# Where a block's statistics stand, and which engine fills its buffers with ones

## The chip, the cores and the metric

The kernel runs on one core of a Trainium2 chip. A core has five engines with a queue of their own each, and each works its queue off in order: TensorE (PE, with the weight loads shown apart as PEld), VectorE (DVE), ScalarE (ACT), GpSimd (POOL) and SyncE (SP, which here only issues transfers). They wait for each other by semaphores. The metric is the device time of one execution in microseconds. Three runs of the kernel before took 902.11 to 902.88 us, median 902.47.

## The reference

The input x has 2 batches of 2048 rows of 256 features, all in float32. Each row is normalised, and an attention and a spectral layer, both of the normalised row, are added to it:

```python
xn = _layernorm(x, axis=-1)
x = x + _L0_attn_ref(xn, wq, wk, wv, wo) + _L0_ffn_ref(xn, w_freq_real, w_freq_imag, bias)
```

The attention has 16 query heads of 16 features and 4 key and value heads, with a rotary embedding on queries and keys and a causal mask:

```python
scores = jnp.einsum('bshd,bthd->bhst', q, k) * scale
scores = jnp.where(causal[None, None, :, :], scores, -jnp.inf)
attn = jax.nn.softmax(scores, axis=-1)
out = jnp.einsum('bhst,bthd->bshd', attn, v).reshape(Bx, Sx, Dx) @ wo
```

The spectral layer is the real part of an inverse FFT of (FFT of xn) times a complex matrix, plus a bias. For a given matrix that is one real 256 x 256 matrix.

## The kernel before, in words

**Blocks and units.** The rows are cut into 8 blocks of 512. The blocks of the two batches alternate: block 0 and block 1 are the first 512 rows of either batch, block 2 and 3 the second, and so on. A unit is one block with one group of 4 query heads, one for each key head, so there are 32 units. Units 0 to 3 belong to block 0, 4 to 7 to block 1, 8 to 11 to block 2. Because of the causal mask later blocks see more key blocks, and their units are longer.

**The way of one block to its scores.** `load_x` brings in the rows (tile `xt`, four row tiles of 128). `row_stats` takes mean and variance of one row tile on VectorE with two instructions (`bn_stats`, `bn_aggr`; lines 283 and 284, tiles `bn` and `mv`). `row_power` makes 1/sqrt(variance + eps) on GpSimd (lines 289, 290, tile `rs`), `row_shift` the shift on VectorE (line 295, tile `sh`). `norm` applies both, four instructions (line 445). `transpose_x` turns the rows over on TensorE (banks `ps_x`, copied by ScalarE to `xnT`), `features` multiplies with the weights (banks `ps_q`, copied to `raw`), for the keys and values first (c = 2), then for two halves of the queries (c = 0 and 1). `other_half` swaps the halves of each head for the rotation: for blocks 0 and 1 by a product (banks `ps_sw`), from block 2 on by transfers. `rotate` and `split` are seven instructions for each c: three for the rotation with the table `cs`, four that split the result into three bf16 parts (tile `part`: high, middle, low). For block 0 they run on VectorE, for the other blocks on GpSimd; the same holds for `norm`. `stack` and `stack_runs` copy the parts by transfers from SyncE's queue (line 439) into `kst` (keys) and `qst` (queries of a unit), seven times 16 partitions, so that one bf16 product over 112 partitions adds up the products of parts.

**Ones.** `ones(n)` fills two buffers of block n before they are partly overwritten: `va[n]` with 1.0 (line 419; values overwrite half of the columns, and a column of ones gives the softmax sums), and the partitions 96 to 127 of `kst[n]` with -1.0, one instruction for each of the four key heads (line 422; the rows 112 to 114 subtract the row maxima).

**The two passes.** First come the row maxima of a unit (`maxima`): TensorE makes score tiles (banks `sm` for whole key blocks, `sd` for the diagonal one, in a ring of two), and VectorE reduces them (line 681), the last of a unit followed by `parts` (lines 792 to 808, tile `np_of`), which turns the maxima into bf16 parts. `spread` brings them to the stacked queries. Then `scores` makes transposed scores with the maximum already taken off (banks `st` or `sp`), ScalarE takes the exponential (line 952, tile `es`), `values` multiplies with `va` (bank `av`), and sums and products go through memory (`put`, `gather`, `widen`) to `output`.

**The spectral matrix.** `spectral_matrix` makes the real matrix on TensorE from tables that `load_late` brings in by GpSimd's queue: four pieces `left` (banks `ps_ff`), then two `right` (banks `ps_mff`).

**What sets the order.** The program is written out at build time by a planner. It keeps a clock for each engine in `clock`, and the time at which each thing will be there in `there`. `use(engine, us, needs, gives)` advances a clock. Work that is not scores, values or maxima stands in `streams`, lists of pieces with the engine, what they need, and two places in the order (from when they may and by when they should be issued). The loop at the end picks what can start soonest, by these estimates, and prefers late maxima. A piece whose needs are not yet in `there` is not picked. So a change of one estimate or one need can change the order in which all engines get their work. At run time only this order and the semaphores count.

**The start.** Before the loop, 48 idle transposes go to TensorE, then the planner's clocks are set (line 1226), and block 0 gets its ones, statistics, `row_power`, the loads of `load_late`, the rotary table (`rotary_table`, line 339) and its shift. `chain(n, ...)` puts the pieces of block n into streams; for blocks 0 and 1 and for block 2's load they may be issued at once. The statistics of block 2 may be issued early too, as its place in the order is before the start:

Of the kernel before, what the change touches and what calls it, by code (L numbers as in the profile page):

```python
# [23 lines left out]
def tile_attn_plus_spectral_ffn(  # L24
# [29 lines left out]
    nc = tc.nc  # L54
# [35 lines left out]
    clock = {e: 0.0 for e in ("pe", "dve", "act", "pool", "sp")}  # L90
# [36 lines left out]
    def use(eng, us, needs=(), gives=()):  # L127
        clock[eng] = max(clock[eng], ready(needs)) + us
        if eng == "pe":
            at = issued[0] // LOADED  # L130
            for k in range(max(loaded), at + 1):
                clock["pe"] = max(clock["pe"], loaded[k])
                loaded[k + 1] = clock["pe"] + LOAD
            clock["pe"] = max(clock["pe"], loaded[at])
        for k in gives:
            there[k] = clock[eng] + LATE[eng]
# [46 lines left out]
    xt = {}  # L183

    def load_x(n):
        at = slot("xt")
        take_slot("xt")
        xt[n] = work.tile([P, NI, D], F32, tag="xt", bufs=2, name=f"xt{n}")
        step = NI if n else 1
        for i in range(0, NI, step):  # L190
            send("sp", 128 * step, [at], [("xt", "in", n, k) for k in range(i, i + step)])
            nc.sync.dma_start(out=xt[n][:, i : i + step, :], in_=block_rows(n)[:, i : i + step, :])
# [86 lines left out]
    def row_stats(n, i):  # L279
        if i == 0:  # L280
            mv[n] = work.tile([P, NI, 2], F32, tag="mv", bufs=2, name=f"mv{n}")
        st = work.tile([P, 6], F32, tag="bn", bufs=3, name=f"bn{n}_{i}")
        nc.vector.bn_stats(st, xt[n][:, i, :])
        nc.vector.bn_aggr(mv[n][:, i, :], st)
        use("dve", 0.6, [("xt", "in", n, i)], [("mv", n)])

    def row_power(n):
        rstd[n] = work.tile([P, NI], F32, tag="rs", bufs=2, name=f"rs{n}")
        nc.gpsimd.tensor_scalar(rstd[n], mv[n][:, :, 1], EPS, None, ALU.add)
        nc.gpsimd.tensor_tensor(rstd[n], rstd[n], neg_half, ALU.pow)  # L290
        use("pool", 1.6, [("mv", n)], [("rs", n)])

    def row_shift(n):
        shift[n] = work.tile([P, NI], F32, tag="sh", bufs=2, name=f"sh{n}")
        nc.vector.scalar_tensor_tensor(
            shift[n], mv[n][:, :, 0], -1.0, rstd[n], ALU.mult, ALU.mult
        )
        use("dve", 0.2, [("rs", n)], [("sh", n)])
# [115 lines left out]
    xnT, va, kst, qst = {}, {}, {}, {}  # L414

    def ones(n):
        e, eng, us = (nc.vector, "dve", 2.7) if n == 0 else (nc.gpsimd, "pool", 2.9)
        va[n] = const.tile([P, NI, NKV, QD], F32, tag=f"va{n}", name=f"va{n}")
        e.memset(va[n], 1.0)
        kst[n] = const.tile([P, NKV, SB], BF16, tag=f"kst{n}", name=f"kst{n}")  # L420
        for h in range(NKV):
            e.memset(kst[n][96:P, h, :], -1.0)
        use(eng, us, (), [("ones", n)])
# [791 lines left out]
    def stream(pieces, since=-1, by=-1):  # L1215
        streams.append([(since, by, *p) for p in pieces])
        return streams[-1]
# [5 lines left out]
    for _ in range(48):  # L1223
        transpose(idle[:, 0:P], ident, ident)
    use("pe", 9.0, (), [("st", k)])
    clock["dve"], clock["act"], clock["pool"] = 1.8, 3.7, 1.8
    ones(0)
    for i in range(NI):
        row_stats(0, i)
# [7 lines left out]
    def chain(n, starts, late=0):  # L1237

        norms, pe, rot = project(n)
        eng = norms[0][0]  # L1240
        stats = [("dve", [("xt", "in", n, i)], [], lambda i=i: row_stats(n, i)) for i in range(NI)]
        stats.append(("pool", [("mv", n)], [], lambda: row_power(n)))
        stats.append(("dve", [("rs", n)], [], lambda: row_shift(n)))
        s = starts
        if n > 1:
            stream([("sp", [], ["xt"], lambda: load_x(n))], s["load"], s["load"])
        if n:
            norm_1 = [("xn", 1, NI - 1)]
            stream([("pool", norm_1, [], lambda: ones(n))], s["ones"], s["stats"])
            stream(stats, s["stats"], s["stats"] + late + 1)  # L1250
        out_pe = streams.append([]) or streams[-1]
        for k, p in enumerate(pe):
            at = s["pe"] + (k // 2 if n > 1 else 0)
            out_pe.append((at, at + late + 1, *p))
        out_rot = streams.append([]) or streams[-1]
        for p in norms:
            out_rot.append((s["stats"], s["stats"] + late + 2, *p))
        for c, more in ((K, 0), (Q0, 2), (Q1, 5)):
            at = s["rot"] + (more if n > 1 else 0)
            for k, p in enumerate(rot[c]):  # L1260
                out_rot.append((at, at + late + 2 + k // 2, *p))
# [10 lines left out]
    early = dict.fromkeys(("load", "ones", "stats", "pe", "rot"), -1)  # L1272
    table(0, -1)
    chain(0, early, -9)
    chain(1, early, 1)
    load_x_2 = stream([("sp", [], ["xt"], lambda: load_x(2))])

# [5 lines left out]
    for n in range(2, NB):  # L1283
        at = next(k for k, d in enumerate(due) if d >= a_from[NG * n])
        starts = dict(load=at - 30, stats=at - 24, pe=at - 20, rot=at - 17)
        starts["ones"] = 0 if n < 4 else 8 * n - 26
        if n == 2:
            starts["load"] = -1
        if n % B == 0:
            table(n // B, max(at - 22, 2))  # L1290
        chain(n, starts)
# [65 lines left out]
    while True:  # L1357
# [4 lines left out]
        if now < NS:  # L1362
            u, t = steps[now]
            h = b_next % NKV
            n, g = units[u]
# [20 lines left out]
        for s in streams:  # L1386
            if s and (s[0][0] <= now or now >= NS):
                since, by, eng, needs, rings, what = s[0]
# [11 lines left out]
        if others and min(others, key=lambda c: c[0])[0] <= limit:  # L1400
            soonest = min(others, key=lambda c: c[0])
            eng = soonest[1][0][2]
# [12 lines left out]
        act, dve = clock["act"] - pe, clock["dve"] - pe  # L1415
# [21 lines left out]
        if kind == "B":  # L1437
# [3 lines left out]
            if b_next % NKV == 0 and first[u + 1] == now + 1:  # L1441
                n, g = units[u]
# [71 lines left out]
```

## Time and profile before

| | |
|---|---|
| median of three runs | 902.47 us |
| the profiled execution | 901.48 us, its span 899.8 us |
| PE busy | 881.7 us, 98% |
| DVE busy | 731.0 us, 81% |
| ACT busy | 638.1 us, 71% |
| POOL busy | 363.3 us, 40% |
| chain that ended last | PE 88%, DVE 8%, ACT 2% |

All times in the profile are microseconds from the start of the span. A line of the timeline gives start, duration, engine, source line, operation and tiles; several alike are merged with a count, and the bracket tells how long the engine had been idle and what ended that. In the table by stage each engine's busy time in a stretch is followed by its number of instructions; the last three columns are the granted clock of TensorE, the busy share of the DMA engines and GB/s. The chain that ended last is followed backwards from the last instruction, at each step to what released it. Matmuls overlap in the pipeline and their ends are modelled, so a full PE need not be a PE at its peak. The granted clock is 1.00 in all stretches.

### The profile page before, as it was taken

What the parts mean: (1) busy time and instruction counts of PE and PEld (TensorE: products, weight loads), DVE (VectorE), ACT (ScalarE), POOL (GpSimd) and SP (SyncE); (2) the same over time, 40 slices, a digit from 0 to 9 for tenths busy, and PEclk for the clock granted to TensorE, in tenths of its full rate; (3) what the DMA queues carried; (4) which work ended last, traced back from release to release, by engine and by line L of the source; (5) the groups of instructions that cost most, each with busy time, mean ns of one, the idle gap of its engine ahead of it and who ended that gap; (6) DMA issues with size and microseconds to landing.
All of it is one profiled execution on the core that took longest, in us unless ns stands there. A gap on an engine that the chain in (4) does not pass through costs nothing.

```text
span 899.8 us, 37181 instructions
## 1 busy us (share of the span) xinstructions
PE 881.7 (98%) x16620; PEld 477.7 (53%) x16620; DVE 731.0 (81%) x1007; ACT 638.1 (71%) x1191; POOL 363.3 (40%) x486
## 2 busy tenths in 40 slices
PE   8899899999999999999999999999999999999998
PEld 5467664555555555555555555555455554545443
DVE  8886997968879996899987899979889989798501
ACT  3365756857767883978964987858597887579885
POOL 6968467725842325712255431212651111101111
PEclk9999999999999999999999999999999999999999
DMA  5446523531343012430012610010143001100000
GB/s 170 116 136 171 148 87 101 134 108 45 79 139 94 29 40 58 128 106 15 15 45 70 167 40 14 26 39 14 53 108 74 14 3 39 50 14 15 27 2 25
DMA packets 42063, 62.02 MB, mean 69 GB/s; under 512 B 8920, under 2 KB 32200, under 8 KB 41904
## 3 DMA queue, kind: packets, MB, share of 16 engines
q1 hardware_dynamic: 32480, 41.18, 16.9%
q0 software_dynamic: 8128, 17.69, 6.2%
q8 instruction: 130, 2.13, 1.0%
q10 hardware_dynamic: 1296, 0.79, 0.3%
q14 instruction: 29, 0.24, 0.1%
HBM read 32.75 MB, written 18.40 MB: 57 GB/s over the span
## 4 chain that ended last, share of the span: by engine, by line
PE 88%; DVE 8%; ACT 2%; issue 1%; POOL 0%; ACTq 0%; POOLq 0%; DVEq 0%
PE av L121 25%; PE st L121 23%; PE sm L121 18%; PE sd L121 7%; PE po L121 6%; PE ps_q L121 4%; DVE top_g L681 2%; PE sp L121 2%; DVE mx L681 2%; ACT es L952 2%; PE ps_ff L121 1%; PE ps_x L125 1%; DVE np_of L808 1%; PE ps_m L121 0%; PE ps_sw L121 0%
## 5 line engine op out<-in xcount | busy, mean ns | idle before, releaser
L952 ACT ACTIVATE es<-st 128x512 f32<-128x512 f32 x1006 | 532.1, 607 | 142.7 <-PE st L121 122.5
L681 DVE TENSOR_REDUCE mx<-sm 128x2 f32<-128x1024 f32 x384 | 450.2, 1218 | 40.9 <-PE sm L121 39.9
L121 PE MATMUL st<-qst,kst 115*32 115x512 bf16 (+9 forms) x4744 | 340.0, 345 | 0.5 <-issue 0.2
L121 PE MATMUL av<-es,va 128*32 128x512 f32 (+3 forms) x2560 | 288.2, 529 | 0.4 <-ACT avs L1033 0.2
L121 PE MATMUL sm<-kst,qst 112*32 112x512 bf16 x3072 | 236.1, 379 | 1.5 <-DVE mx L681 0.8
L121 PEld LDWEIGHTS <-kst 115*32 115x32 bf16 x5120 | 162.4, 95 | 141.4 <-issue 64.6
L121 PEld LDWEIGHTS <-qst 112*32 112x32 bf16 x5632 | 151.7, 96 | 127.3 <-issue 81.2
L681 DVE TENSOR_REDUCE top_g<-sd 128x25 f32<-128x800 f32 (+1 forms) x192 | 168.3, 906 | 39.3 <-PE sd L121 38.8
L970 POOL TENSOR_SCALAR_AFFINE_SELECT es<-es 128x512 f32<-128x512 f32 (+1 forms) x120 | 65.3, 546 | 240.1 <-ACT es L952 239.9
L121 PEld LDWEIGHTS av<-es,va 128*32 128x32 f32 x2560 | 82.4, 109 | 46.7 <-issue 18.3
L121 PE MATMUL sd<-kst,qst 112*32 112x384 bf16 (+11 forms) x2560 | 101.6, 256 | 1.6 <-DVE top_g L681 1.4
L1044 POOL DMA_DIRECT2D res<-avs x30 | 18.0, 599 | 109.9 <-ACT avs L1023 109.9
L121 PEld LDWEIGHTS <-ident_h 128*32 128x32 bf16 x1344 | 47.4, 96 | 28.1 <-issue 21.9
L1158 DVE TENSOR_TENSOR xr<-po,xr 128x256 f32<-128x256 f32 x36 | 15.2, 424 | 48.8 <-PE po L121 48.3
L121 PE MATMUL sd<-mask,ident_h 128*32 128x64 bf16 x1024 | 53.7, 193 | 0.8 <-DVE mx L681 0.5
L121 PE MATMUL ps_q<-xnT,wp 128*32 128x512 f32 x384 | 47.3, 594 | 0.2 <-ACT xnT L460 0.2
L475 ACT COPY raw<-ps_q 128x512 f32<-128x512 f32 x24 | 14.1, 586 | 44.4 <-PE ps_q L121 42.8
L952 ACT ACTIVATE es<-sp 128x1024 f32<-128x1024 f32 x41 | 39.7, 1028 | 6.1 <-PE sp L121 5.9
L566 POOL TENSOR_TENSOR ra<-raw,cs 128x512 f32<-128x512 f32 (+1 forms) x21 | 27.3, 1300 | 20.1 <-ACT raw L475 19.2
L121 PE MATMUL po<-wo_sb,attT 128*32 128x256 f32 x512 | 34.3, 380 | 0.0
L121 PE MATMUL po<-mff,xnT 128*32 128x256 f32 x512 | 33.7, 379 | 0.0
L1069 POOL DMA_DIRECT2D sums<-den x15 | 8.1, 540 | 53.7 <-DVE den L1063 53.7
(115 smaller groups left out, 625.1 us busy)
## 6 DMA issues: line engine op xcount, KB each, us to landing
qst<-run SPq DMA_DIRECT2D x62, 128.0 KB
res<-avs POOLq DMA_DIRECT2D x30, 256.0 KB, 2.9
run<-part SPq DMA_DIRECT2D x31, 192.0 KB
qst<-run SPq DMA_DIRECT2D x31, 192.0 KB
xr<-in_L_attn_x_dram SPq DMA_DIRECT2D x16, 256.0 KB
sw<-raw SPq DMA_DIRECT2D x60, 64.0 KB
attT<-res POOLq DMA_DIRECT2D x15, 256.0 KB, 4.2
inv<-sums POOLq DMA_DIRECT2D x15, 256.0 KB, 3.7
```

What stands on the lines that cost most here:

```text
L121: nc.tensor.matmul(to, lhsT, rhs, **more)
L125: nc.tensor.transpose(to, of, unit)
L475: nc.scalar.copy(raw[c], ps)
L566: e.tensor_tensor(ra[c][:r], raw[c][:r], cs[j][:r, 0, :], ALU.mult)
L681: nc.vector.tensor_reduce(out, of, AX.X, ALU.max)
L808: nc.vector.tensor_reduce(to, of, AX.X, op, negate=negate)
L952: nc.scalar.activation(to, of, AF.Exp, scale=SCALE)
L970: nc.gpsimd.affine_select(out=to, in_=to, pattern=pattern, compare_op=ALU.is_ge, fill=0.0, base=0, channel_multiplier=-1,)
L1044: nc.gpsimd.dma_start(out=res[n, c][f], in_=avs[u])
L1069: nc.gpsimd.dma_start(out=sums, in_=den[n, c])
L1158: nc.vector.tensor_tensor(xr[n, r][:, e, :], po, xr[n, r][:, e, :], ALU.add)
```

## The change

Three things are changed. `ones(0)` runs on GpSimd, as it does for the other blocks, with an estimate of 2.5 us. The planner's clocks of VectorE and GpSimd at the start are set to 3.0 and 3.5 instead of 1.8. And the first row tile's statistics of block 2 need the maxima of the first unit, `("np", 0, 0)`, which are there after `parts` of unit 0; the other three row tiles stand behind it in the same stream. No computation is added or left out.

```diff
     def ones(n):
-        e, eng, us = (nc.vector, "dve", 2.7) if n == 0 else (nc.gpsimd, "pool", 2.9)
+        e, eng, us = nc.gpsimd, "pool", 2.5 if n == 0 else 2.9
...
-    clock["dve"], clock["act"], clock["pool"] = 1.8, 3.7, 1.8
+    clock["dve"], clock["act"], clock["pool"] = 3.0, 3.7, 3.5
     ones(0)
...
         stats = [("dve", [("xt", "in", n, i)], [], lambda i=i: row_stats(n, i)) for i in range(NI)]
+        if n == 2:
+            stats[0] = ("dve", [("xt", "in", n, 0), ("np", 0, 0)], [], lambda: row_stats(n, 0))
         stats.append(("pool", [("mv", n)], [], lambda: row_power(n)))
```

In the built program the order then differs from before in these places. On VectorE the five fills are gone, and the eight statistics instructions of block 2 stand between the first maxima of unit 1. On GpSimd the five fills stand ahead of block 0's `row_power`; block 2's `row_power` stands behind the first half of block 1's queries, its `norm` inside the second half. On TensorE block 2's `transpose_x` stands among the maxima of unit 2 instead of ahead of the first maxima, and the four `ps_ff` pieces stand one ahead of `ps_sw` of block 1's keys, one among unit 0's maxima, one in unit 1's and one in unit 2's; before, two stood in units 0 and 1 and two behind unit 4's. Later differences are exchanges of neighbours, and from the fourth key tile of unit 16 on the order on TensorE is the same.

## The prediction

> **What bounds the kernel now.** I read the page's shares first, then busy time by stage, then the start instruction by instruction, then the chain of waits.
>
> ```profile
> PE 881.7 (98%) x16620; PEld 477.7 (53%) x16620; DVE 731.0 (81%) x1007; ACT 638.1 (71%) x1191; POOL 363.3 (40%) x486
> ```
>
> Busy time by stage (columns: stretch, length, then PE, PEld, DVE, ACT, POOL):
>
> ```profile
> 0.00:31.00 31.00, 25.55 (x192) 13.86 (x196) 26.15 (x74) 11.65 (x23) 23.55 (x45) 1.00 0.46 147
> 33.00:65.00 32.00, 29.77 (x845) 20.33 (x841) 28.77 (x62) 17.99 (x35) 25.64 (x30) 1.00 0.49 136
> 65.00:82.00 17.00, 17.00 (x417) 13.03 (x414) 8.28 (x16) 8.40 (x18) 14.65 (x15) 1.00 0.47 124
> 320.00:850.00 530.00, 529.34 (x9508) 274.96 (x9501) 458.01 (x544) 399.51 (x757) 159.63 (x211) 1.00 0.18 49
> ```
>
> From 320 on PE runs without a gap, so its work sets the time; what can be won lies before. In 0 to 31 PE holds 7.3 us of idle transposes and long waits; in 33 to 65 DVE (28.77 of 32) and PE take turns; in 65 to 82 PE is full and DVE half idle. The timeline of the start (start, duration, engine, line, instruction, idle before):
>
> ```profile
> 3.16 0.48 DVE L419 MEMSET va<- 128x512 f32 x1
> 3.81 2.11 DVE L422 MEMSET kst<- 32x512 bf16 x4 [0.16 <-issue]
> 5.94 0.43 DVE L283 BATCH_NORM_STATS2 bn<-xt 128x6 f32<-128x256 f32 x1
> ...
> 8.27 0.24 POOL L289 TENSOR_SCALAR rs<-mv 128x4 f32<-128x4 f32 x1 [4.83 <-DVE mv L284]
> ...
> 9.88 1.57 DVE L445 TENSOR_SCALAR xt<-xt,rs,sh 128x256 f32<-128x256 f32 x4
> ...
> 18.42 0.92 DVE L596 TENSOR_TENSOR rb<-raw,part 64x512 f32<-64x512 f32 x1
> ...
> 19.27 0.41 DVE L283 BATCH_NORM_STATS2 bn<-xt 128x6 f32<-128x256 f32 x1
> ...
> 21.40 0.39 DVE L599 CAST part<-rb 64x512 bf16<-64x512 f32 x1
> ...
> 29.87 1.38 DVE L590 CAST part<-raw 128x512 bf16<-128x512 f32 x1
> ...
> 33.21 3.31 DVE L681 TENSOR_REDUCE top_g<-sd 128x18 f32<-128x576 f32 x4
> ```
>
> To see: DVE fills until 5.92 and only then takes block 0's statistics, while POOL idles 4.83; at 19.27 block 2's statistics cut block 0's K split (rb, then the cast) in two; the first maximum waits until DVE has split the last Q at 33.29. The chain of waits shows what PE does later when it is full:
>
> ```profile
> 72.70 3.50 PE ps_ff L121 x62
> ```
>
> **The change part by part.** The profiled execution took 901.48 us: span 899.8 and 1.7 around it. That is 0.99 under the median of the runs, 902.47, so a difference worked out against it is taken off the median.
>
> *Fills to POOL.* DVE loses 0.48 + 2.11 us. Its next instruction waits for data: the trace's semaphore updates put the landings of block 0's four row tiles at 3.05, 3.83, 5.59 and 6.05, and of the rotary table at 6.59. At a pitch of 0.53 (6.41 to 6.94, mv to mv) the statistics now end near 6.75 instead of 8.17: 1.4, not 2.6. POOL is free at 3.44 and needs 0.52 + 1.91 (the fills at 18.76) to 0.80 + 2.20 (those at 30.91), so until 5.9 to 6.5, before the statistics end; nothing queued behind it (rstd, then six table loads, then block 1's rstd) waits longer; the loads come 1.4 earlier with rstd, and the last table that the early spectral piece needs (landed 18.79) was in time anyway. Were this cover gone, each us late would move rstd. Rstd, shift and the normalisation come 1.4 earlier. PE's idle transposes end only at 8.70, so the turning of the rotary table gains 0.7, but the transposes of x wait for the last normalised tile and gain all; ACT's copies in between cost 0.1. I take 1.3. Ends: 0.7 (that turning gates) and 1.4.
>
> *Block 2's statistics away from the start.* Eight instructions leave between 19.34 (end of rb) and 21.40: 2.06, and block 2's shift at 23.8 (0.07 on the chain): 2.1. The chain of waits puts ACT's raw at 22.01 ahead of DVE's ra at 22.61. But that ra waits for ACT's 13th semaphore update, the raw copy of 18.52, done by 19.11; DVE is gapless from 17.0. So all 2.1 is on the path, and with the 1.3 the first maximum goes from 33.21 to 29.8. Data and PE must be there: the last of Q0's seven stack transfers landed at 31.40 and goes 3.4 earlier with its source, to 28.0; SP's stacks keep their order. PE went from 20.04 (ps_q) to 30.89 (first sd); in the new order block 2's two transposes with their waits (2.15) leave and a spectral piece (1.75, of which 0.75 fills the wait before ps_sw) comes in: 18.7 + 9.7 = 28.4. DVE still decides.
>
> *The statistics put back.* In the built order they stand between the maxima of unit 1: 2.1 there (2.3 by 4 x (0.40 + 0.18)). DVE waits 0.42 + 0.59 us for PE in that unit, so 1.1 to 2.3; I take 2.1, because DVE is the busier engine. DVE's net by the end of unit 3 is 1.3.
>
> *What moves with it.* POOL: block 2's rstd and normalisation leave the place before block 1's rotation; that starts when its raw comes (about 25.6 instead of 29.27), and its K stack issues on SP 5 us earlier. Rstd now stands behind Q0's split and the normalisation inside Q1's, and costs Q1's stacks nothing, since they end earlier than before. PE: of four ps_ff pieces two stood before unit 3's maxima ended; now all four do. The last two (3.50 at 72.70) leave the stretch 65 to 82 where PE is full, and DVE, 8.28 of 17 busy, can follow: 3.5 gained, if they cost nothing earlier. In the stretch of units 0 to 3 PE gets one piece more than it had (1.75) and block 2's transposes (0.66 x 2): 3.1. There is room for 32.00 - 29.77 = 2.2, and 2.1 more because DVE's stretch is longer: 4.3. It does not all lie where the pieces stand, so I let a quarter not fit, 0.8 (ends 0 and 3.1).
>
> How full PE is there could be read otherwise. Weight loads are busy 20.33 of 32 us in that stretch (64%) and 274.96 of 530 (52%) later. The Trainium skill (Perfetto Trace Analysis, Identifying the Most-Contended Engine) judges TensorE's headroom by that share, not by matmul busy time: by it this stretch has less room than the full one, the pieces would not fit, and the sum would be 1.3 instead of 4.0. I go by the waits, because the maxima here use many short matmuls (845 in 32 us against 9508 in 530), each with its load.
>
> *Neighbours.* Some DVE instructions are stretched while POOL works: the cast at 29.87 took 1.38 against 0.54 at 24.66, L604 0.92 against 0.69, two at 27.5 and 29.0 0.17 more each: 1.4 in all. POOL's work beside them changes. Bounds: 1.4 won, 0.5 lost (a fill of 0.48 ahead of one cast); I take 0, since fills take the place. The Trainium skill (SBUF — State Buffer, Who interferes with whom) says a DVE cast in a two-port mode and a GpSimd instruction exclude each other, whichever starts second waiting; by it the fills can stop the casts, and the sum would be 3.5.
>
> *Sum:* 1.3 + 2.1 - 2.1 + 3.5 - 0.8 = 4.0 us; 901.48 - 4.0 = 897.5 for the profiled execution, 902.47 - 4.0 = 898.5 for the median. From unit 16's fourth key tile (its first exp is at 310) the instruction order on PE is the same to the end, so what is won by then stays. Between 105 and 320 the order shifts here and there; PE idles 0.9 + 1.0 there, which bounds that at about 1 us either way.
>
> **The rivals.**
> - *Only the head counts* (the pieces don't fit, or PE gives the 3.5 back): gain 1.3, ends 0.5 and 2.3; 901.2. For it: PE busy 93% in 33 to 65; the reading by weight loads leads here. Against: DVE's 90% there, and it gets 2.1 more.
> - *Block 2's transposes stall PE: slower.* They stand in PE's queue ahead of unit 2's last maxima; behind them wait all sd, scores and so DVE. Their normalisation follows on POOL: statistics end near 42.6, rstd 1.5, three rotations 3.9, then 2.2 to 3.1: 50.2 to 51.1. PE gets there about 51.0 (unit 2's first maximum 49.0, two tiles on). On time by a hair; DVE has 1.9 us of queued tiles as cushion. Beyond that each us costs one, and from about 57 all of the gain is gone; 6 us beyond that cushion gives 902.47 - 4.0 + 6 = 904.5. Against: POOL's rows from 34 on are even (1.16 to 1.31).
> - *Washed out later* by the changed order between 105 and 320, or the stats hide less: about 902.0.
> - *More than forecast*: all pieces fit and half the stretched DVE time goes: 4.0 + 0.8 + 0.7 = 5.5; 897.0.
>
> **How the numbers follow.** 0.2% is 1.8 us, about what a measurement of this kernel can tell. Forecast 0.60 (gain 3 to 5), more 0.08, head only 0.17 (0.05 over 1.8, 0.12 within), washed out 0.07 (0.05 within, 0.02 slower), stall 0.08. Faster 0.60 + 0.08 + 0.05 = 0.73, same 0.17, slower 0.10. The range 896.8 to 901.9 leaves out the stall, the lower end of head only and a little below: 0.17.
>
> **What would show it.** Right: the first bn of block 0 near 3.2 and rstd near 6.9; cast directly behind rb near 18.0; first maximum near 29.8; the statistics between unit 1's maxima; no ps_ff after 60; unit 4's first exp (92.3 before) about 4 earlier, unit 16's likewise. Wrong: a PE wait for POOL's xt near 51; DVE idle before the first maximum; PE idle in 33 to 65 not smaller.

## The result and the profile after

The changed kernel takes 897.45 us (median of 5 runs, 896.71 to 898.69); the kernel before, on the same chip, 902.88 (902.11 to 905.04). The ratio is 0.9935, 95% interval 0.9919 to 0.9951: 5.9 us less by the ratio, 5.4 by the medians. A second measurement on another occasion gave 0.9942 (0.9921 to 0.9962). The forecast was 4.0 us less, and 897.45 lies near the lower end of its range. The profiled execution took 896.71 us with a span of 895.0, 4.8 less than the span before. It was the quickest of its five, as the profiled one of before was quicker than all that were timed beside it in that measurement.

The page's shares:

```profile
PE 879.4 (98%) x16620; PEld 481.8 (54%) x16620; DVE 730.8 (82%) x1002; ACT 638.3 (71%) x1191; POOL 365.0 (41%) x491
```

Busy time by stage of the changed kernel (stretch, length, PE, PEld, DVE, ACT, POOL, then granted clock, share of the DMA engines, GB/s):

```profile
0.00:31.00 31.00, 26.95 (x272) 15.21 (x273) 25.25 (x63) 11.03 (x23) 27.04 (x50) 1.00 0.50 154
...
33.00:65.00 32.00, 30.88 (x843) 22.15 (x843) 28.87 (x66) 17.85 (x36) 23.20 (x29) 1.00 0.59 146
65.00:82.00 17.00, 16.91 (x480) 12.46 (x469) 11.10 (x21) 10.47 (x22) 13.74 (x14) 1.00 0.38 102
82.00:105.00 23.00, 21.65 (x650) 15.01 (x648) 20.73 (x40) 15.49 (x30) 16.68 (x21) 1.00 0.69 204
...
320.00:850.00 530.00, 528.67 (x9496) 275.60 (x9491) 453.41 (x536) 400.08 (x754) 159.09 (x211) 1.00 0.17 49
```

The row of before that the prediction did not show:

```profile
82.00:105.00 23.00, 20.44 (x636) 14.26 (x629) 20.13 (x40) 15.15 (x30) 15.07 (x20) 1.00 0.73 207
```

PE is fuller by 1.4 us in 0 to 31 (in 31 to 33 it idles as much more: it is busy for 0.62 of 2 us instead of 2.00, while it waits for the first maximum), by 1.1 in 33 to 65 and by 1.2 in 82 to 105. In 65 to 82, where it was full before and is now, VectorE has 11.10 us of work instead of 8.28: the maxima go on there where PE had been doing the spectral pieces.

The start of the changed kernel in the timeline (start, duration, engine, line, instruction, and in brackets the idle time before it and what ended that):

```profile
3.07 0.43 DVE L283 BATCH_NORM_STATS2 bn<-xt 128x6 f32<-128x256 f32 x1
...
3.98 1.92 POOL L422 MEMSET kst<- 32x512 bf16 x4
...
5.29 0.43 DVE L283 BATCH_NORM_STATS2 bn<-xt 128x6 f32<-128x256 f32 x1 [0.86 <-DMA xt<-in_L_attn_x_dram]
...
7.06 0.25 POOL L289 TENSOR_SCALAR rs<-mv 128x4 f32<-128x4 f32 x1 [1.17 <-DVE mv L284]
...
8.68 1.57 DVE L445 TENSOR_SCALAR xt<-xt,rs,sh 128x256 f32<-128x256 f32 x4
...
17.21 0.92 DVE L596 TENSOR_TENSOR rb<-raw,part 64x512 f32<-64x512 f32 x1
18.16 0.76 DVE L599 CAST part<-rb 64x512 bf16<-64x512 f32 x1
...
25.97 1.46 POOL L566 TENSOR_TENSOR ra<-raw,cs 64x512 f32<-64x512 f32 x1
26.34 1.38 DVE L590 CAST part<-raw 128x512 bf16<-128x512 f32 x1
...
27.79 1.78 POOL L569 TENSOR_TENSOR sw<-sw,cs 64x512 f32<-64x512 f32 x1 [0.36 <-DVE part L590]
28.48 1.37 DVE L599 CAST part<-rb 128x512 bf16<-128x512 f32 x1
29.64 1.35 POOL L574 TENSOR_TENSOR raw<-ra,sw 64x512 f32<-64x512 f32 x1
29.88 1.67 DVE L604 TENSOR_TENSOR part<-rb,part 128x512 bf16<-128x512 f32 x1
...
31.47 3.30 DVE L681 TENSOR_REDUCE top_g<-sd 128x18 f32<-128x576 f32 x4
```

To see: the fills run on POOL and end before it is needed; VectorE takes its statistics at once and then waits for the rows themselves (0.86 at 5.29). The normalisation starts at 8.68 instead of 9.88. The cast that stood at 21.40 stands at 18.16, directly behind `rb`. So up to there 3.2 us are won. At the first maximum only 1.7 are left (31.47 against 33.21): in the last split of block 0 the two casts take 1.38 and 1.37 and the last subtraction 1.67, where before they took 1.38, 0.56 and 0.69. Block 1's rotation on POOL now lies beside them from 25.97; before it started at 29.27, behind block 2's normalisation, and lay beside the first cast alone. The rows of before:

```profile
29.27 1.69 POOL L566 TENSOR_TENSOR ra<-raw,cs 64x512 f32<-64x512 f32 x1
...
32.01 0.56 DVE L599 CAST part<-rb 128x512 bf16<-128x512 f32 x1
32.60 0.69 DVE L604 TENSOR_TENSOR part<-rb,part 128x512 bf16<-128x512 f32 x1
```

Block 2's statistics stand where the planner puts them now, between unit 1's maxima:

```profile
39.10 0.75 DVE L681 TENSOR_REDUCE top_g<-sd 128x18 f32<-128x576 f32 x1
39.77 0.42 DVE L283 BATCH_NORM_STATS2 bn<-xt 128x6 f32<-128x256 f32 x1
40.22 0.18 DVE L284 BATCH_NORM_AGGREGATE mv<-bn 128x2 f32<-128x6 f32 x1
...
48.37 0.92 DVE L295 SCALAR_TENSOR_TENSOR sh<-mv,rs 128x4 f32<-128x4 f32 x1
```

The spectral pieces by tile (duration min/median/max in ns, first and last start in us), of before:

```profile
L121 PE MATMUL ps_ff<-dc,wre x32: 377/379/383, 35.1 to 73.3; 128*32 128x256 f32 x32
L121 PE MATMUL ps_ff<-neg_s,wre x32: 379/379/379, 43.6 to 75.8; 128*32 128x256 f32 x32
```

and of the changed kernel, where all four are done by 53:

```profile
L121 PE MATMUL ps_ff<-dc,wre x32: 377/379/382, 24.3 to 41.4; 128*32 128x256 f32 x32
L121 PE MATMUL ps_ff<-neg_s,wre x32: 379/379/379, 34.2 to 52.0; 128*32 128x256 f32 x32
```

The two `right` pieces of the matrix (`ps_mff`) move as well, from behind unit 5's first score tile to the place ahead of it that the last `ps_ff` pieces have left. First before, then the changed kernel:

```profile
L121 PE MATMUL ps_mff<-dc,at__353 x32: 378/379/403, 76.4 to 78.9; 128*32 128x256 f32 x32
...
L121 PE MATMUL ps_mff<-dc,at__348 x32: 377/379/382, 73.6 to 76.0; 128*32 128x256 f32 x32
```

How the lead develops is best read at marks that every kernel has: the first maximum of a unit, or its first exponential. All are starts in us after the span's, and for the other kernels the difference to before. "Apart" and "held" are experiments told below.

| mark | before | after | apart | held |
|---|---|---|---|---|
| first maximum, unit 0 | 33.21 | -1.74 | -3.56 | -1.51 |
| unit 1 | 40.84 | -1.74 | -3.54 | +0.12 |
| unit 2 | 50.29 | +0.47 | -1.05 | +0.89 |
| unit 5 | 76.76 | +1.05 | -0.03 | +2.23 |
| unit 6 | 87.00 | -2.51 | -3.58 | +1.68 |
| unit 8 | 103.15 | -3.44 | -4.82 | +0.84 |
| first exponential, unit 4 | 92.31 | -3.62 | -4.65 | +1.21 |
| unit 16 | 309.76 | -5.07 | -6.48 | -0.56 |
| span | 899.76 | -4.77 | -6.24 | +0.10 |

The column of "after" has the whole story. 1.7 us are won before the first maximum, 2.2 are given back for the statistics in unit 1, 0.6 more go by unit 5, and then 3.6 are won at once between unit 5 and unit 6. The last two `ps_ff` pieces had stood a little ahead of that, from 72.5 on, before unit 5's first maximum; the win shows only behind this mark because the two `ps_mff` pieces, as long, have moved in front of it. Another 2.3 come afterwards, all of them by unit 16.

### The profile page after: what moved, and what is told of

It reads as the page before. It is cut to its first block, busy times and chain, and to the rows that moved or that the text cites. A ratio compares the mean times of both kernels' runs of the same rounds, so it can differ in the third digit from the quotient of the medians.

```text
span 895.0 us, 37152 instructions
## 1 busy us (share of the span) xinstructions
PE 879.4 (98%) x16620; PEld 481.8 (54%) x16620; DVE 730.8 (82%) x1002; ACT 638.3 (71%) x1191; POOL 365.0 (41%) x491
## 4 chain that ended last, share of the span: by engine, by line
PE 88%; DVE 7%; ACT 3%; DMA 1%; issue 1%; SPq 0%; ACTq 0%; DVEq 0%
PE av L121 25%; PE st L121 24%; PE sm L121 18%; PE sd L121 7%; PE po L121 6%; PE ps_q L121 4%; ACT es L952 2%; DVE top_g L681 2%; PE sp L121 2%; DVE mx L681 1%; DMA qst<-mt 1%; PE ps_x L125 1%; PE ps_m L121 0%; DMA trig<-rope_dram 0%; DVE np_of L808 0%
## 5 line engine op out<-in xcount | busy, mean ns | idle before, releaser
L121 PE MATMUL st<-qst,kst 115*32 115x512 bf16 (+8 forms) x4744 | 340.5, 345 | 1.3 <-DMA qst<-mt 0.5
L121 PEld LDWEIGHTS <-kst 115*32 115x32 bf16 x5120 | 164.2, 95 | 139.2 <-issue 62.3
L827 ACT CAST mt<-ps_m 12x512 bf16<-12x512 f32 x32 | 18.3, 571 | 19.1 <-PE ps_m L121 18.6
```

The source lines that it names most:

```text
L121: nc.tensor.matmul(to, lhsT, rhs, **more)
L827: nc.scalar.copy(mt, ps[0 : 3 * NKV, :SB])
```

## The experiments

My theory after this reading: the gain is (a) a shorter head, of which a good half is lost again because POOL and VectorE stretch each other, and (b) room for two more spectral pieces ahead of 65 us. The rivals: that the head alone counts; that the pieces could have been placed there without moving anything; that the stretched split is an accident of one execution.

**Only the fills.**

```diff
-        e, eng, us = (nc.vector, "dve", 2.7) if n == 0 else (nc.gpsimd, "pool", 2.9)
+        e, eng, us = nc.gpsimd, "pool", 2.5 if n == 0 else 2.9
...
-    clock["dve"], clock["act"], clock["pool"] = 1.8, 3.7, 1.8
+    clock["dve"], clock["act"], clock["pool"] = 3.0, 3.7, 3.5
```

> The fills of block 0 on GpSimd and the planner's two start clocks, block 2's statistics left where they were; TensorE's order is then that of the kernel before, to the end. My theory (each part counts by itself: 1.3 for the fills, the rest for what the move of the statistics does to the order): first maximum at 31.9 instead of 33.2, unit 4's first exp 1.3 earlier, span 898.5 against 899.8. Rival (all of the gain is order, the head is swallowed by later waits): first maximum 31.9, but unit 4's exp and the span within 0.4 of before.

902.19 us against 902.67 (this and the next two, and the one kept apart below, were measured together), ratio 0.9993 (0.9981 to 1.0004): smaller than expected, and by the times not told from nothing. The trace has the 1.3 us where they were put: the normalisation starts at 8.56 instead of 9.88. At the first maximum 0.98 is left, as one cast of the last split takes 1.85 instead of 1.38; this lead is still there at unit 4's first exponential (0.96), and the span is 1.6 shorter.

**Only the statistics.**

```diff
+        if n == 2:
+            stats[0] = ("dve", [("xt", "in", n, 0), ("np", 0, 0)], [], lambda: row_stats(n, 0))
```

> Block 2's statistics behind unit 0's maxima, the fills left on VectorE; TensorE's order is then that of the changed kernel, to the end. My theory: the changed kernel's gain less 1.3, so a span of 896.3. Rival (order alone): 895.0 to 895.4, the whole gain. If block 1's rotation on GpSimd stretches block 0's last split, as in the changed kernel (casts of 1.37 and 1.38, L604 1.67), the first maximum is at 32.8 to 33.2, hardly earlier than before, although the statistics have left.

899.14 us, ratio 0.9958 (0.9943 to 0.9973). PE's order is that of the changed kernel to the end. So this part carries most of the gain. Its first maximum is at 32.68, only 0.5 earlier than before: the same three stretched instructions (1.38, 1.38 and 1.67) are in its last split. Its span, 897.4, is 1.1 above what I had expected; it has a stretch of slower TensorE clock that is told below.

**Pieces early, nothing moved.**

```diff
-        for needs, piece in spectral_matrix():
-            spectral_pieces.append((-1, 8, "pe", needs, ["st"], piece))
+        for k, (needs, piece) in enumerate(spectral_matrix()):
+            spectral_pieces.append((-1, 3 if k < 4 else 8, "pe", needs, ["st"], piece))
```

> The kernel before, fills and statistics in their old places, with the four spectral pieces due by step 3 instead of 8: the last two ps_ff pieces then stand among unit 2's maxima instead of behind unit 4's. My theory (these two are 3.5 of the 4.8 us, PE has room for them there): first maximum unchanged at 33.2, unit 3's maxima less than 1 later, unit 4's exp 2.5 to 3.5 earlier, span 896.3 to 897.3. Rival (the room comes from moving the statistics; without it the pieces delay the maxima by their own length): units 2 and 3 later by 2 to 3.5, span 899 to 900.

901.93 us, ratio 0.9984 (0.9973 to 0.9995): 1.4 us by the times, a good third of what the statistics gave. Its profiled execution shows no gain: all four pieces are done by 58 us, but the units between are late by about what they cost (unit 5's first maximum +5.05, of which 0.96 is a late start), and the 2.9 won at unit 6 do not quite pay that back. The start was late because block 2's statistics, still in the head, waited 0.51 for their rows, and because the first cast of the last split took 1.84. The span, 900.9, is above both what I and what the rival expected. The places are not quite those of the changed kernel either: there one piece stands at 24.3, in the head, where block 2's transposes have left room, and here the first starts at 36.0. So two more pieces ahead of 65 us are worth little by themselves; with VectorE's lighter start they are worth more.

**Pieces held back in the changed kernel.** The last two `ps_ff` pieces may only come from step 8 of the planner on, as they did before, and block 2's products from step 6 on, so that they don't fill the place instead.

```diff
-        for needs, piece in spectral_matrix():
-            spectral_pieces.append((-1, 8, "pe", needs, ["st"], piece))
+        for k, (needs, piece) in enumerate(spectral_matrix()):
+            spectral_pieces.append((8 if k == 2 else -1, 8, "pe", needs, ["st"], piece))
...
             at = s["pe"] + (k // 2 if n > 1 else 0)
+            if n == 2 and k > 1:
+                at = max(at, 6)
```

> The changed kernel, but the last two ps_ff pieces may be issued from step 8 on, as far back as before the change, and block 2's features from step 6 on, so that they don't fill the gap; both stand behind unit 4's first maxima again, the rest of the order of units 0 to 4 is nearly that of the changed kernel. My theory (the two pieces hidden in units 1 and 2 are most of the gain): the first maxima of units 1 to 3 0 to 0.8 earlier than in the changed kernel, those of unit 6 (the third of block 1) and all after it 2.7 to 3.5 later, span 897.7 to 898.5, so 1.2 to 2 under the kernel before. Rival (the gain is the head and the later order): within 1 of the changed kernel.

901.60 us against 903.08 (this one, the same wait in the kernel before, and the two with the statistics later were measured together), ratio 0.9981 (0.9970 to 0.9992). Against the changed kernel's two ratios that is 3.5 to 4.2 us lost. The spectral tile in its profile:

```profile
L121 PE MATMUL ps_ff<-dc,wre x32: 379/379/403, 24.5 to 75.4; 128*32 128x256 f32 x32
...
L121 PE MATMUL ps_ff<-neg_s,wre x32: 379/506/634, 34.8 to 78.0; 128*32 128x256 f32 x32
```

Two pieces are back in the full stretch, and the table shows the effect: this kernel's first maximum comes like the changed one's (0.23 apart), it is still level in unit 3 (0.10), and 4.2 us behind it at unit 6's first maximum, 4.9 at the end. The profile is worse than I had expected, though (897.7 to 898.5), and units 1 to 3 came later, not earlier. Part of that is a stretch of half clock from 34.0 to 37.4, which the first profile of the changed kernel does not have (the pieces in it are the ones that took up to 634 ns); it is explained below. The second profile of the changed kernel has it too, and against that one this kernel starts 1.1 earlier (31.70 against 32.83), is 2.3 ahead in unit 3 and 2.0 behind at the end. So holding back wins about 1.1 by unit 3 and loses 4.3 behind it, 3.1 us net. The edit also puts block 2's products and transposes later, and with them many later neighbours, so the share of the pieces alone is not told apart; where the lead goes, ahead of unit 6, speaks for them. With the run before it, the theory fits: it takes both, the place and the room.

**POOL kept off the split.** The changed kernel, with a cast of one column of block 0's last part on GpSimd ahead of block 1's rotation. It is otherwise useless, and makes the rotation wait until VectorE's split is done; the planner is told of it by the need.

```diff
+            if n == 1 and c == NK and k == 0:
+                held_back = work.tile([P, 1], F32, tag="hb", bufs=1, name="hb")
+                nc.gpsimd.tensor_copy(held_back, last_part[0][:, 2, 0:1])
...
+                if n == 0 and c == 1:
+                    last_part.append(part[c])
...
-                (eng, [("raw", "in", n, c), ("cs", j, 0)], [], lambda c=c: rotate(c, 0)),
+                (eng, [("raw", "in", n, c), ("cs", j, 0)] + [("part", "in", 0, 1, "l")] * (n == 1 and c == NK),
+                 [], lambda c=c: rotate(c, 0)),
```

> The changed kernel with one more GpSimd instruction ahead of block 1's rotation: it copies one column of block 0's last bf16 part, so the rotation can start only when VectorE has split the last queries; TensorE's order is that of the changed kernel. Theory (neighbours: VectorE's last split was stretched by GpSimd's rotation): L599 and L604 of that split fall from 1.37 and 1.67 to about 0.5 and 0.7, first maximum near 29.8 instead of 31.47, and if VectorE bounds the first units, the span falls by up to 1.7 to 893.3. Rival (the stretch has another cause): both stay over 1.3, first maximum at 31.5, and GpSimd's later rotation costs 0 to 2.

896.19 us, ratio 0.9929 (0.9911 to 0.9947) to the 902.67. VectorE's queue in its timeline (line numbers are a few higher through the edit):

```profile
27.01 0.43 DVE L596 CAST part<-raw 128x512 bf16<-128x512 f32 x1
27.47 0.69 DVE L602 TENSOR_TENSOR rb<-raw,part 128x512 f32<-128x512 f32 x1
28.20 0.43 DVE L605 CAST part<-rb 128x512 bf16<-128x512 f32 x1
28.66 0.69 DVE L610 TENSOR_TENSOR part<-rb,part 128x512 bf16<-128x512 f32 x1
29.65 1.42 DVE L688 TENSOR_REDUCE top_g<-sd 128x18 f32<-128x576 f32 x2 [0.29 <-PE sd L121]
```

and POOL's:

```profile
29.50 0.19 POOL L567 CAST hb<-part 128x1 f32<-128x1 bf16 x1 [3.51 <-DVE part L610]
29.65 1.27 POOL L570 TENSOR_TENSOR ra<-raw,cs 64x512 f32<-64x512 f32 x1
```

POOL now idles 3.51 us and starts its rotation 3.7 later, and yet the first maximum comes 1.8 earlier, at 29.65. The two casts are at 0.43 and the subtraction at 0.69. 1.5 us of it are left at the end of the profiles. The stretching is real. Its three rows add up to 2.87 us; 1.8 of these show at the first maximum, since this split started 0.67 later (an earlier cast, beside GpSimd's fills, took 1.21 instead of 0.76) and VectorE then waited 0.29 for PE's first tile.

**The same wait in the kernel before**, whose own last split has one stretched cast.

> The kernel before with the same GpSimd wait as in the run that kept GpSimd's rotation away from VectorE's last split, and nothing else; order as before. Theory (neighbours cost VectorE 0.8 to 1.3 here too: the cast of 1.38 falls to 0.54): first maximum 0.8 to 1.3 earlier, and since VectorE's lead lasts (the fills' 0.96 lasted to unit 4), span 0.6 to 1.3 less. Rival (VectorE's head start of one us is lost to run-to-run differences, or GpSimd's rotation, 4 later, holds up block 1): no gain, or up to 1 slower.

902.05 us, ratio 0.9986 (0.9975 to 0.9997): 1.3 us, as expected, with an interval from 0.3 to 2.3: the small edit seems to help the old kernel too. The cast of 1.38 fell to 0.76, not to 0.54. But the first maximum of the profiled execution is 1.07 later than before and its span 1.1 longer, since it was late by something else. VectorE's timeline there:

```profile
21.05 0.43 DVE L283 BATCH_NORM_STATS2 bn<-xt 128x6 f32<-128x256 f32 x1 [1.71 <-DMA xt<-in_L_attn_x_dram]
```

Block 2's rows landed late and VectorE waited 1.71 us for them in the middle of block 0's split. In the profiles of before and of the fills alone this wait was nil, in that of the early pieces 0.51. The moved statistics come some 20 us later and do not meet it.

**Statistics later still**, on top of the kernel kept apart: behind unit 1's maxima, then behind unit 2's.

```diff
-            stats[0] = ("dve", [("xt", "in", n, 0), ("np", 0, 0)], [], lambda: row_stats(n, 0))
+            stats[0] = ("dve", [("xt", "in", n, 0), ("np", 0, 1)], [], lambda: row_stats(n, 0))
```

> The run with the GpSimd wait (span 893.5), with block 2's statistics behind unit 1's maxima instead of unit 0's; the planner then puts block 2's transposes into unit 3 and the last ps_ff piece behind unit 4. Theory (VectorE bounds units 0 to 3, so the statistics cost 2.1 there wherever they stand, and each piece that goes back behind unit 4 costs 1.75): unit 1's last maxima 2 earlier, unit 3's the same again, one piece lost: span 894.5 to 896. Rival (later is better, since TensorE is full from unit 4 on): 891 to 893.

898.75 us, ratio 0.9958 (0.9942 to 0.9974).

> As the last, with the statistics behind unit 2's maxima: they then fall near 63, and block 2's transposes and features come behind unit 4's and unit 5's maxima, near 75 to 85. Theory: VectorE reaches the end of unit 2 2 earlier than with the statistics ahead, but GpSimd needs 22 us for block 2's rotation and splits, so its first stack lands near 100 to 105, when unit 8's maxima are due (98): TensorE or VectorE waits, span 895 to 899. Rival (the wait is filled by other units): 891 to 893.

With `("np", 0, 2)`: 902.39 us, ratio 1.0004 (0.9987 to 1.0020). The first was in the expected range, the second is worse than I expected. Up to unit 6 it is ahead of the kernel before by 3.7 us; at unit 8's first maximum 1.1 are left and at its first exponential nothing (+0.36). Its stages there:

```profile
105.00:127.00 22.00, 17.68 (x464) 10.56 (x457) 18.14 (x25) 12.21 (x24) 15.50 (x27) 1.00 0.40 115
127.00:131.00 4.00, 3.83 (x80) 2.23 (x83) 2.68 (x5) 2.17 (x4) 2.92 (x5) 0.57 0.62 184
```

PE idles 4.3 us of 22, where the changed kernel idles 0.8 of the same 22. So "later" is not better. Nearly all of these 4.3 are waits that ended with one of VectorE's maxima (0.85 and 0.97 the longest). That block 2's own units are the next to need what hangs on the statistics is likely, and not shown.

**Changed and apart once more, side by side.**

> The changed kernel once more, unaltered, beside the next one on one chip. My theory: 5.0 to 5.9 us below the kernel before (ratio 0.9935 to 0.9945), a profiled span near 895.0 with the first maximum near 31.5 and unit 4's first exponential near 88.7. The rival, that part of the first measurement's gain was the luck of that chip and that the profile's 4.8 is all there is: 4.5 to 4.9 below the kernel before.

> The changed kernel with the one-column cast on GpSimd behind the last part of block 0's split, as in e4_apart, beside the changed kernel on one chip. My theory, that the two engines stretch each other by 1.8 us at the end of the head and that the lead is kept: span near 893.5, first maximum near 29.7, and 1.0 to 1.8 us below the median of e9_after_again. The rival, that what is won before the first maximum is lost in the spread of executions: within 0.5 us of e9_after_again.

899.13 us (897.15 to 900.07) and 896.88 (896.01 to 899.06), against 903.99: ratios 0.9942 (0.9921 to 0.9962) and 0.9926 (0.9908 to 0.9945). 2.25 us between the medians, 1.4 by the ratios, with intervals that overlap; the two pairs of measurements and the two pairs of profiles all put the one kept apart ahead. It is the best version found. Its first maximum was at 29.47.

The profile of the changed kernel was 2.9 us longer this time. 1.36 of it are there at the first maximum: the first rotation started 0.41 later, and other instructions were stretched: block 0's second key cast took 1.22 instead of 0.76, and in its last rotation and split three took 1.61, 1.76 and 1.40. The rest has a cause that I had not thought of. PE's timeline behind the stretched split, and the stage after it:

```profile
33.63 0.35 PE L121 MATMUL sd<-kst,qst 112*32 112x384 bf16 x4 [2.51 <-DVE top_g L681]
```

```profile
34.00:38.00 4.00, 3.90 (x58) 2.42 (x52) 2.17 (x3) 0.00 (x0) 3.00 (x3) 0.57 0.64 167
```

PE waited 2.51 us for VectorE's first maximum (in the first profile 1.45), and then its granted clock was 0.5 for 3.4 us: the mean over these four is 0.57. That alone delays unit 1's first maximum by 1.7, from 1.36 behind the first profile to 3.04. The same dip follows a wait of 2.06 in the profile of the statistics alone and of 2.04 in that of the held pieces; none follows 1.45 or less, nor a wait of 1.72 at 99.3 in the second profile of the kernel kept apart. A dip of that length makes a mean clock of 0.998 over the execution, and each timed execution has its mean clock on record, though not the place of its dips. 8 of 11 executions of the changed kernel are at 0.998 or below, 10 of 81 of the kernel before, 3 of 12 of the kernel kept apart. So I tested the wait itself, in both directions.

**PE kept busy in that wait.** The changed kernel with twelve idle transposes ahead of the third tile.

```diff
                     begin()
+                    if (n, g, h) == (0, 0, 0):
+                        more = bank("more")
+                        there["st", take_slot("st")] = clock["pe"]
+                        for _ in range(12):
+                            nc.tensor.transpose(more[:, 0:P], ident, ident)
                     pair_of(f"sd{n}_{g}_1_{h}")
```

> The changed kernel with twelve idle transposes on TensorE (about 0.15 us each by the 48 at the start, 1.8 in all) ahead of the third tile of unit 0's first maxima, where TensorE waited 1.45 us for VectorE in the first profile and 2.51 in the second. The order is the same otherwise. My theory: a wait of about 2 us or more there makes the clock go to half for 3.4 us, and 8 of 11 executions of the changed kernel paid it; with the transposes the wait is under 1 us, most executions have a mean clock of 0.999 or 1.0, and the median is 0.5 to 1.5 us below the changed kernel's, against the kernel before a ratio of 0.9925 to 0.994, though the transposes themselves can cost 0.4. The rival, that the half clock comes by chance and not from the wait: still most executions at 0.998, a ratio of 0.994 to 0.9945.

897.93 us against 903.00, ratio 0.9946 (0.9932 to 0.9960). PE in its timeline:

```profile
29.78 1.53 PE L757 MATMUL more<-ident 128*128 128x128 f32 x12
31.85 0.35 PE L121 MATMUL sd<-kst,qst 112*32 112x384 bf16 x4 [0.54 <-DVE top_g L681]
```

**The opposite**: the kernel kept apart, with 25 memsets on VectorE between the split and the first maximum.

```diff
                 if e == 1:
+                    if (n, g, pr) == (0, 0, 0):
+                        pause = work.tile([P, P], F32, tag="pause", bufs=1, name="pause")
+                        for _ in range(25):
+                            nc.vector.memset(pause, 0.0)
                     on_dve(
```

> The opposite: the kernel with the one-column cast (e4_apart, 9 of 12 executions at a mean clock of 0.999 or 1.0) with 25 small memsets on VectorE, about 3.6 us, between the end of block 0's split and the first maximum. GpSimd does not overlap the split, the order is the same. First maximum near 32.5 to 33; TensorE waits about 2.5 us ahead of its third tile. My theory: half clock for 3.4 us behind it in most executions, mean clock 0.998, and the median 4 to 5 us above the one without the pause: 3 for the later start and 1 to 1.5 for the clock; ratio to the kernel before 0.997 to 0.998. The rival, that the half clock is chance or belongs to GpSimd's overlap: most executions at 0.999 or 1.0 and at most 3 us above.

902.18 us, ratio 0.9988 (0.9977 to 0.9999). The memsets took 0.25 us each, 6.37 in all, more than I had estimated, so that PE waited longer:

```profile
35.62 0.51 PE L121 MATMUL sd<-kst,qst 112*32 112x384 bf16 x4 [5.29 <-DVE top_g L688]
```

The clock answers both ways: with the transposes all 5 executions are at 1.0, with the pause all 11 are at 0.998 or below, 9 of them at 0.996 or less (half clock from 33.0 to 39.9 in its profile). The half clock belongs to PE's wait, and needs no GpSimd. What it costs in the changed kernel is less clear. I had expected the kept-busy kernel to be 0.5 to 1.5 us quicker, and it is not: its first maximum comes 0.4 earlier than the changed kernel's in the first profile, but it loses 0.8 between unit 2 and unit 3 and 0.7 later for reasons that I did not follow. The 12 executions of the held-back kernel differ by 1.5 us between those at 1.0 (mean 900.5) and those at 0.998 (902.0); in the second measurement of the changed kernel the difference is 0.3. In the kernel kept apart it is 3.4 and 2.2 in the two measurements, with three executions at 0.998. About a microsecond or more is likely, and not shown.

The pause also gives an upper price of time in the head: the first maximum is 5.4 later than in the kernel without it (34.88 against 29.47), the span 6.7, and the half clock of 6.8 us is in that.

## Why the prediction was right, point by point

The direction and the size were right, and so was the mechanism that carries most of it. But two terms were wrong by about 1.5 us or more each, in opposite directions, and the agreement of the sum (4.0 forecast, 4.8 in the profile, 5.4 in the medians) owes something to that: it is partly luck.

- *Fills, 1.3:* right. 1.2 at the normalisation in the changed kernel, 1.3 with the fills alone. The limit by landings held: statistics end at 6.87 (forecast 6.75), with waits of 0.86 and 0.29 for the rows. (The landing at 18.79 belongs to `wo`; the last table that the early spectral piece needs landed at 17.98, in time as well.)
- *Statistics out of the head, 2.1, all on the path:* right. The cast directly behind `rb` stands 3.24 earlier (forecast 3.4 with the fills), and where the last split is not stretched the first maximum is at 29.65 and 29.47, for a forecast of 29.8. What decides there is not VectorE, as forecast, but PE's first tile, for which VectorE waits 0.29 and 0.60: the queries' stack was forecast to land at 28.0, but PE's first products with it start at 29.16 in the changed kernel (after 0.69 of waiting for it), at 29.12 and 28.95 in the two profiles of the kernel kept apart. The changed kernel, late through the stretching, does not feel this.
- *Neighbours, 0, at most 0.5 lost:* **wrong, the step that failed.** Of 3.24 us won up to the cast at 18.16, 1.74 were left at the first maximum, and with the overlap gone it comes 1.8 us earlier in the first pair of profiles and 3.4 in the second (29.47 against 32.83). I had looked at a fill as the instruction beside the last split, and a few lines above had put the start of block 1's rotation at 25.6. These two belonged together: the rotation, which block 2's normalisation had kept away, now lies beside the split. The Trainium skill (SBUF — State Buffer, Who interferes with whom) states not only the rule for casts that I cited, but also that a VectorE instruction with two inputs in SBUF contends with a GpSimd instruction that reads SBUF. The trace agrees: the cast at 26.34 ends 0.29 behind the GpSimd product that had started ahead of it, the one at 28.48 0.28 behind the next, the subtraction at 29.88 0.56 behind the third. The fills of later blocks had a share too: the cast at 18.16 lies beside them and took 0.76, against 0.39 before.
- *Statistics put back, 2.1:* right as a sum, 2.2 between the first maxima of units 1 and 2. It is made up otherwise: the eight instructions take about 2.2, block 2's shift at 48.37 adds 0.8, as it took 0.92 instead of 0.15 beside a GpSimd product, and VectorE waits 0.5 less for PE in that unit (0.52 instead of 1.01); the rest are small differences.
- *Pieces out of the full stretch, 3.5:* right, 3.6 between units 5 and 6, and 3.5 to 4.2 us in the times when they are held back (with block 2's products).
- *A quarter not fitting, 0.8:* right, 0.6 by unit 5, and 1.1 by unit 3 against the held-back kernel. The reading by weight loads would have had the pieces not fit at all. Their share in 33 to 65 even rose from 20.33 to 22.15 of 32, and PE's busy time with it. Used to compare two stretches, as the prediction used it, the measure of the Trainium skill (Perfetto Trace Analysis, Identifying the Most-Contended Engine) and the trace differ here, and the waits were the better guide.
- *Later order, 1 either way:* **too small.** Between unit 6 and unit 16 2.6 more were won, and 2.1 with the statistics alone. I had bounded this by PE's idle time between 105 and 320, and had left out 82 to 105, where PE idled 2.6 us before. It idles 1.35 there now. That is not all of it: 0.9 of the 2.6 came by unit 8's first maximum, near 100, and 1.6 behind it, while PE's idle time between 105 and 320 fell only from 1.92 to 1.34. Part of it is the marks themselves, which move with the order of the maxima: counted by the work that PE has done (an estimate from the trace, by matmul columns, fp32 columns twice and those of transposes ten times), the lead is about 3.4 us near 80, 3.8 near 130 and 5.0 near 280, so some 1.6 come later and not 2.6. Which exchange of neighbours did it stays open.
- *The rivals:* "head only" fell with the held-back pieces; "washed out later" was the wrong sign. Block 2's transposes did not stall: the normalisation ended at 51.5, a little later than forecast, but PE came to them at 53.05 and not at 51. In the kernel kept apart, where PE comes at 51.2 and POOL is later, they did wait, 0.21 us twice. So the margin was thin, and its price there is small.
- *The granted clock* was in no term. At a full clock the changed kernel's profile gains 4.8; the medians contain the dips of both kernels and the late landings that the moved statistics no longer meet. How much of the 0.6 us between medians and profile is which was not measured.

## What to carry to other kernels

When work leaves a queue, look at what moves up into the freed time on the *other* engine, and lay the two timelines side by side at their new places: here the gain on VectorE pulled GpSimd's work under VectorE's critical split, and one tiny instruction that makes it wait won back 1.5 us in the first pair of profiles (3.6 in the second, with the half clock in it); by the times the two kernels are 0.5 to 1.4 us apart, within their intervals. A gain in a stage that one engine bounds can be worth more by the work of another engine that now fits there; ask what stands in a later, full stretch and could be done in the new gap. And when terms are summed, look at each stretch once: one left out (82 to 105 here) can hold as much as a term that was worked out.

## What the runs showed of the hardware

- *TensorE's clock fell to half after a wait of about 2 us.* Waits of 2.04, 2.06 and 2.51 us were each followed by about 3.4 us at 0.5, beginning 3.3 to 3.6 us after the wait began; after 1.72, 1.45, 1.19 and 0.82 the clock stayed at 1.00. With a wait of 5.29 the half clock began 2.7 after its start and lasted 6.8. One long wait is not needed: with the statistics last, a dip came at 127.3 where the 3.4 us ahead of it held several waits of at most 0.66, 1.7 us in all; elsewhere 1.8 us in 3.4 (one wait of 1.72) brought none, so no sharp limit is shown. Ahead of the other dips PE had idled 2.0 to 2.7 of the last 3.4 us. The Trainium skill (TensorE: Matmul & The Clock Gate, Part 1) says that the clock falls after an idle window of about 3.4 us and rises after a busy one. The length of the dips agrees; the idle time that brings them on was shorter here.
- *The landing of the same rows scatters.* Block 2's first row tile was waited for by 0, 0, 0.51 and 1.71 us at nearly the same place of kernels that load it alike.
- *A small memset is not cheap in proportion.* 128 x 128 floats took 0.25 us each back to back on VectorE, where 128 x 512, four times as many, took 0.48.
